# Moving small vector work of a two-layer network to POOL and ACT, and normalising attention for all heads at once

## The chip, the cores and the metric

The kernel runs on one core of a Trainium2 chip. Its engines work side by side, each through its own queue in a fixed order: TensorE (PE), VectorE (DVE), ScalarE (ACT), GpSimd (POOL) and SyncE (SP, which here issues most of the DMAs). They wait for each other through semaphores. The metric is the device time of one launch in microseconds. A time is a median of several runs; beside it stands one execution taken with the hardware profiler, from which all durations of single instructions come.

## The reference

Input x is 4 sequences of 512 tokens with 128 features, float32. Four blocks follow, each added to x after a layer norm:

```
x = x + L0_attn(layernorm(x))   # Mamba block, then causal attention (4 heads of 32, 2 KV heads), then gated FFN
x = x + L0_ffn(layernorm(x))    # 128 -> 512 with ternary weights, gelu, layer norm over 512, 512 -> 128
x = x + L1_attn(layernorm(x))   # a second Mamba block
x = x + L1_ffn(layernorm(x))    # router over 8 experts, top 1, gated FFN of width 512
```

A Mamba block projects to 2 x 256 channels, runs a convolution over 4 tokens, computes `delta = softplus(...)`, B and C, and then the selective scan over time for 16 states of each of 256 channels: `h = exp(delta * A) * h + delta * B * x`, `y = sum over states of h * C`. Then y is gated with `silu(z)` and projected back.

The norms: `layernorm(x) = (x - mean) / sqrt(var + 1e-5)`, `rmsnorm(x) = x / sqrt(mean(x^2) + 1e-6)`. Attention is `softmax(q k^T * scale, causal) v`.

## The kernel before

Four sequences (b = 0 to 3) are worked on as 4 tiles of 128 tokens each. The stages of a sequence are generators: `front0` (two norms, convolution, gate, B/C, softplus), `scan0` (16 jobs, each of two states of one half of the channels), `first` (back projection and attention), `dense` (gated FFN, then `bitffn` with ternary weights), `front1` and `scan1` for the second Mamba block, `second` (back projection and router), and then `sort` and `experts` for the sequences (0, 1), (2) and (3). `run` gives every stage a due time and `collect` draws steps from the generators in order of these.

Nothing is issued at once. Every call on an engine goes to `Plan.call`, which notes it with a cost from `Plan.cost` and its dependencies. `Plan.order` then lays out the queues of all engines: it takes, again and again, the instruction that can start first by its own model of time (within 0.1 us, the one that is due first), with room in the buffer rings taken into account and 1.35 us for a change of ACT's function table. `issue` emits the program in that order. So other operations or costs give another order in every queue. All planned instructions show as line 201 of the profile (the helper that emits them); the table loads are line 336, the scatters of rows line 1093.

A scan job (`scan_states`): PE spreads a row of B over all partitions into PSUM (`b_n<-parts,sel`), DVE multiplies it by `du` (`b_n<-b_n,du`), ACT makes the decay (`decay<-delta,nega`), DVE runs the scan (`hs<-decay,b_n`), POOL multiplies by C (`hs<-hs,rep`) and, in the first layer and for b below 2 in the second, adds the two states (`hs<-hs`); PE sums over states (`y<-hs,ident`). The decay has three buffers, `hs` four, the PSUM ring `mm` four.

The parts that the change touches:

- Norms: `moments` takes mean and variance on DVE, `rstd` raises `var + eps` to the power -1/2 on POOL, `shifted` makes the offset `-mean * r` on DVE (`nm_r<-mv,r`) and applies both on ACT. `two_norms` chains two of these, with three small DVE products (`ms`, `rr`) between.
- The end of `front`: B and C rows are split in bf16 parts (`parts`, `rest`), with a cast on DVE. Then softplus of v is computed as max(v, 0) plus log(1 + e) with e = exp(-|v|), where the logarithm is held within bounds that come from e. The tile `v` is `du` before `du` is made.
- `attention`: for the tile groups (0, 1), (2), (3) and each head, scores, row maximum, exponential, transposes to `tp`, copy to `pT`, product with v into `tp`, whose last column is the sum of the weights (`v` holds a column of ones); then, head by head, a reciprocal `rs` and a product into `o`.
- `bitffn`: gelu on ACT into `g`, its moments on DVE, and the norm over 512 features.

Of the kernel before, what the change touches and what calls it, by code (L numbers as in the profile page):

```python
# [14 lines left out]
AF = mybir.ActivationFunctionType  # L15
ALU = mybir.AluOpType
# [4 lines left out]
P = 128  # L21
B, T, D = 4, 512, 128
NT = T // P
# [3 lines left out]
HEADS, HD = 4, 32  # L27
FFN = 341
FCH = [(0, 128), (128, 128), (256, 85)]
HID, NHC = 512, 4  # L30
# [8 lines left out]
SCL, OFF, PROB, NUM = D, D + 1, D + 2, D + 3  # L39
# [311 lines left out]
class Net:  # L351
# [250 lines left out]
        self.nc.sync.dma_start(out=self.x[b], in_=self.a["x"][b].rearrange("(t p) d -> p t d", p=P))  # L602


    def rstd(self, name, var, eps, r=None):
        nc = self.nc
        r = self.sm("r", [P, NT], bufs=4) if r is None else r
        ve = self.sm("ve", [P, NT], bufs=4)
        nc.gpsimd.tensor_scalar(ve, var, eps, None, ALU.add)
        nc.gpsimd.tensor_tensor(r, ve, self.nhalf, ALU.pow)  # L610
        return r

    def moments(self, name, parts):

        nc = self.nc
        mv = self.sm("mv", [P, NT, 2], bufs=4)
        for t, part in enumerate(parts):
            st = self.sm("st", [P, 6], bufs=4)
            nc.vector.bn_stats(st, part)
            nc.vector.bn_aggr(mv[:, t, :], st)  # L620
        return mv

    def shifted(self, y, x, mean, r, off=None):

        nc = self.nc
        off = self.sm("nm_r", [P, NT], bufs=4) if off is None else off
        nc.vector.scalar_tensor_tensor(off, mean, -1.0, r, ALU.mult, ALU.mult)
        for t in range(NT):
            nc.scalar.activation(
                y[:, t, :], x[:, t, :], AF.Identity, bias=off[:, t:t + 1], scale=r[:, t:t + 1]  # L630
            )
        return y

    def layernorm(self, name, x):
        mv = self.moments(name, [x[:, t, :] for t in range(NT)])
        return self.shifted(self.t4("ln"), x, mv[:, :, 0], self.rstd(name, mv[:, :, 1], 1e-5))

    def two_norms(self, x):

        nc = self.nc  # L640
        mv = self.moments("in", [x[:, t, :] for t in range(NT)])
        r = self.rstd("in", mv[:, :, 1], 1e-5)
        ms = self.sm("ms", [P, NT])
        nc.vector.tensor_tensor(ms, r, r, ALU.mult)
        nc.vector.tensor_tensor(ms, ms, mv[:, :, 1], ALU.mult)
        rr = self.rstd("m", ms, 1e-6)
        nc.vector.tensor_tensor(rr, rr, r, ALU.mult)
        y = self.shifted(self.t4("ln"), x, mv[:, :, 0], rr)
        return self.shifted(self.t4("h", bufs=4), x, mv[:, :, 0], r), y

    def rmsnorm(self, name, x):
        nc = self.nc
        ss = self.sm("ss", [P, NT], bufs=4)
        y = self.t4("ln")
        for t in range(NT):
            nc.scalar.activation(y[:, t, :], x[:, t, :], AF.Square, scale=D ** -0.5, accum_out=ss[:, t:t + 1])
        r = self.rstd(name, ss, 1e-6)
        for t in range(NT):
            nc.scalar.activation(y[:, t, :], x[:, t, :], AF.Identity, scale=r[:, t:t + 1])
        return y  # L660
# [15 lines left out]
    def front(self, b, layer, x, scale=None):  # L676

        nc = self.nc
# [41 lines left out]
        rest = self.ft("rest", [P, T], tag="f", bufs=2)  # L720
        nc.scalar.copy(parts, ps)
        nc.vector.tensor_tensor(rest[64:, :], ps[64:, :], parts[64:, :], ALU.subtract)
        nc.vector.tensor_copy(parts[64:, :], rest[64:, :])
        nc.vector.tensor_tensor(parts[96:, :], rest[96:, :], parts[96:, :], ALU.subtract)

        yield
# [4 lines left out]
        for c in range(NB):  # L731
            ps = self.mm("dl_ps")
            for i in range(NB):
                nc.tensor.matmul(
                    ps, lhsT=step[:, i, c * P:(c + 1) * P], rhs=xs[:, i, :],
                    start=(i == 0), stop=(i == NB - 1),
                )
            nc.scalar.activation(v[:, c, :], ps, AF.Identity, bias=db[:, c:c + 1])
            nc.scalar.activation(e[:, c, :], ps, AF.Abs, bias=db[:, c:c + 1])
        yield  # L740
        nc.scalar.activation(e, e, AF.Exp, scale=-1.0)
        nc.scalar.activation(delta, e, AF.Ln, bias=1.0)
        nc.vector.scalar_tensor_tensor(v, v, 0.0, e, ALU.max, ALU.add)
        nc.gpsimd.tensor_tensor(delta, delta, e, ALU.subtract)
        nc.vector.scalar_tensor_tensor(e, e, -0.5, e, ALU.mult, ALU.mult)
        nc.vector.scalar_tensor_tensor(delta, delta, 0.0, e, ALU.min, ALU.max)
        nc.gpsimd.tensor_tensor(delta, v, delta, ALU.add)
        nc.gpsimd.tensor_tensor(du, delta, xs, ALU.mult)
        yield
        self.m[b] = xs, sz, delta, du, parts, cd  # L750
# [94 lines left out]
    def attention(self, b):  # L845
        nc = self.nc
        h = self.h[b]
        x = self.rmsnorm("a", h)
        xT = self.transposed(x, self.vec("norm_a"))
        qT = self.ft("qT", [P, T], bufs=1)  # L850
        ps = self.mm("q_ps")
# [14 lines left out]

        o = self.ft("o", [P, NT, D], bufs=1)
        turned = []
        for tiles in ((0, 1), (2,), (3,)):
            for hd in range(HEADS):  # L870

                hp, g = slice(hd * HD, (hd + 1) * HD), hd // 2
                at = [0, 1][:len(tiles)]
                ps = self.mm("s_ps")
                pr = self.ft("pr", [P, T], bufs=4)
                nm = self.sm("nm", [P, 2], bufs=4)
# [18 lines left out]
                turned.append(last)  # L895
                pT = self.ft("pT", [P, T], bufs=4)
                nc.scalar.copy(pT[:, :blocks * P], tp[:, :blocks * P])
                w = HD + 1
                for n, i in enumerate(tiles):
                    for j in range(i + 1):  # L900
                        nc.tensor.matmul(
                            tp[:, n * w:(n + 1) * w], lhsT=pT[:, (at[n] + j) * P:(at[n] + j + 1) * P],
                            rhs=v[:, j, g, :], start=(j == 0), stop=(j == i),
                        )
                m = len(tiles)
                po = tp[:, :m * w].rearrange("p (n w) -> p n w", w=w)
                rs = self.sm("rs", [P, 2, 1], bufs=4)
                nc.vector.reciprocal(rs[:, :m, :], po[:, :, HD:])
                nc.vector.tensor_tensor(
                    o[:, tiles[0]:tiles[0] + m, hp], po[:, :, :HD],  # L910
                    rs[:, :m, :].to_broadcast([P, m, HD]), ALU.mult,
                )
                yield
        oT = self.transposed(o)
        ps = self.mm4("oproj_ps")
        for t in range(NT):
# [5 lines left out]
    def ffn(self, b):  # L922
        nc = self.nc
        h = self.h[b]
        xT = self.transposed(self.rmsnorm("f", h), self.vec("norm_f"))
        hT = self.big("hT", [P, len(FCH), T])
        for i, (f0, fn) in enumerate(FCH):
            pg = self.mm("gate_ps")
            nc.tensor.matmul(pg[:fn, :], lhsT=self.wg[:, f0:f0 + fn], rhs=xT, start=True, stop=True)
            pu = self.mm("up_ps")  # L930
            nc.tensor.matmul(pu[:fn, :], lhsT=self.wu[:, f0:f0 + fn], rhs=xT, start=True, stop=True)
            sg = self.ft("sg", [P, T], bufs=1)
            nc.scalar.activation(sg[:fn, :], pg[:fn, :], AF.Silu)
            nc.vector.tensor_tensor(hT[:fn, i, :], sg[:fn, :], pu[:fn, :], ALU.mult)
        yield
        ps = self.mm4("down_ps")
        for t in range(NT):
            for i, (f0, fn) in enumerate(FCH):
                nc.tensor.matmul(
                    ps[:, t, :], lhsT=hT[:fn, i, t * P:(t + 1) * P], rhs=self.wd[:fn, i, :],  # L940
                    start=(i == 0), stop=(i == len(FCH) - 1),
                )
        nc.vector.tensor_tensor(h, h, ps, ALU.add)
        nc.gpsimd.tensor_tensor(self.x[b], self.x[b], h, ALU.add)
        yield

    def bitffn(self, b):
        nc = self.nc
        xT = self.transposed(self.layernorm("b", self.x[b]))
        g = self.big("gelu", [P, NT, HID])  # L950
        for t in range(NT):
            ps = self.mm("fc_ps")
            nc.tensor.matmul(ps, lhsT=xT[:, t * P:(t + 1) * P], rhs=self.wfc, start=True, stop=True)
            nc.scalar.activation(g[:, t, :], ps, AF.Gelu)
        yield
        mv = self.moments("h", [g[:, t, :] for t in range(NT)])
        r = self.rstd("h", mv[:, :, 1], 1e-5)
        self.shifted(g, g, mv[:, :, 0], r)
        gT = self.big("geluT", [P, NHC, T])
        lw, lb = self.vec("lnw"), self.vec("lnb")  # L960
        for c in range(NHC):
            tp = self.mm("tp")
# [14 lines left out]


    def front1(self, b):
        x = self.layernorm("s", self.x[b])  # L980
        yield
        yield from self.front(b, 1, x)

# [7 lines left out]
    def route(self, b):  # L991
# [8 lines left out]
            )  # L1000
        hot, hb = (t[:, ts] for t in self.choice)
        x, row = self.x[b], self.rows_x[b]
        mv = self.moments("e", [x[:, t, :] for t in range(NT)])
        r = self.rstd("e", mv[:, :, 1], 1e-5, row[:, :, SCL])
        ln = self.shifted(self.t4("ln"), x, mv[:, :, 0], r, row[:, :, OFF])
        xT = self.transposed(ln)
        ps = self.mm4("router_ps")
        for t in range(NT):
# [324 lines left out]
```

## Time and profile before

| | |
|---|---|
| median of 3 runs | 954.47 us (954.31 to 960.29) |
| the profiled execution | 953.64 us |
| its span, first to last instruction | 951.8 us |
| mean granted PE clock | 0.874 |
| PE busy | 768.1 us (81%), 3198 matmuls |
| DVE busy | 704.9 us (74%), 1149 instructions |
| POOL busy | 586.9 us (62%), 406 |
| ACT busy | 526.8 us (55%), 916, of them 57 table loads with 73.1 us |
| DMA | 108.70 MB, mean 114 GB/s |

Busy shares are means over stages with different limits; a matmul's end is modelled, so a busy PE is not PE at its peak. In a group's row stand the line, engine and operation, what is written and read, the shapes and the count, then busy time and the mean of one in ns, then the idle time of the engine just before these instructions and what ended it. A stretch row gives start and end, its length, and the busy time and number of instructions of each engine in it, then the granted PE clock and the DMA share. "Idle before" on an engine that is not the bottleneck costs nothing.

### The profile page before, as it was taken

The numbers are of one execution on the slowest core, as the hardware profiler recorded it, in microseconds if no ns is written. First come the engines' busy times: TensorE is split into PE (matmuls) and PEld (weight loads), VectorE is DVE, ScalarE is ACT, GpSimd is POOL, SyncE is SP. The second block draws the span as 40 slices with busy tenths as digits, with TensorE's granted clock in tenths as the row PEclk, the third lists the DMA queues.
The fourth block names the chain that finished last, engine by engine and source line by source line (L and its number), as shares of the span: only waits on it lengthen the run. The fifth ranks groups of instructions, "written<-read, shape, count | busy, mean of one in ns | idle before, by whom it ended". The sixth has DMA issues, their size and how long they took to land. (4 is left out here: it accounts for less than half of the span.)

```text
span 951.8 us, 10451 instructions
## 1 busy us (share of the span) xinstructions
PE 768.1 (81%) x3198; PEld 444.9 (47%) x3225; DVE 704.9 (74%) x1149; ACT 526.8 (55%) x916; POOL 586.9 (62%) x406
## 2 busy tenths in 40 slices
PE   4965669987999887889679998966798988889296
PEld 2411135444544644347225456433345666567185
DVE  5389996688778995787993857599978788787222
ACT  4572346545677565566546756683447556462142
POOL 4279987378666873747792535569758555563222
PEclk9965769978998999789969977978899999799689
DMA  5533343033221221412231204223425797575103
GB/s 164 156 108 110 116 128 111 2 104 109 75 89 46 89 95 38 133 45 67 90 134 43 67 23 155 90 85 129 141 74 188 242 322 244 176 243 183 41 23 93
DMA packets 52694, 108.70 MB, mean 114 GB/s; under 512 B 7700, under 2 KB 21748, under 8 KB 52639
## 3 DMA queue, kind: packets, MB, share of 16 engines
q1 hardware_dynamic: 50942, 105.90, 34.9%
q0 software_dynamic: 1696, 2.14, 0.7%
q8 instruction: 25, 0.41, 0.2%
q14 instruction: 31, 0.25, 0.1%
HBM read 103.12 MB, written 6.27 MB: 115 GB/s over the span
## 5 line engine op out<-in xcount | busy, mean ns | idle before, releaser
L201 POOL TENSOR_TENSOR hs<-hs,rep 128x1024 f32<-128x1024 f32 x126 | 299.4, 2377 | 148.1 <-issue 54.4
L201 DVE TENSOR_TENSOR_SCAN hs<-decay,b_n 128x512 f32<-128x512 f32 x256 | 311.7, 1218 | 18.2 <-ACT decay L201 1.7
L201 ACT ACTIVATE decay<-delta,nega 128x511 f32<-128x511 f32 x256 | 178.3, 718 | 155.7 <-DVE hs L201 146.5
L201 PE MATMUL y<-hs,ident 128*128 128x512 f32 x320 | 194.6, 711 | 20.4 <-POOL hs L201 19.6
L201 DVE TENSOR_TENSOR b_n<-b_n,du 128x512 f32<-128x512 f32 x256 | 173.9, 681 | 31.2 <-PE b_n L201 12.8
L201 PE MATMUL b_n<-parts,sel 128*128 128x512 bf16 x229 | 95.4, 446 | 89.2 <-DVE hs L201 83.2
L201 POOL TENSOR_TENSOR hs<-hs 128x512 f32<-128x512 f32 x96 | 123.3, 1285 | 7.1
L201 PEld LDWEIGHTS y<-hs,ident 128*128 128x128 f32 x320 | 63.0, 218 | 123.7 <-POOL hs L201 91.4
L1093 POOL DMA_INDIRECT out<-yj,xg x37 | 39.3, 1061 | 57.5 <-DVE yj L201 49.9
L336 ACT ACT_TABLE_LOAD x57 | 73.1, 1283 | 1.7 <-PEq L1322 0.8
L201 PEld LDWEIGHTS <-sel 128*128 128x128 bf16 x256 | 28.3, 111 | 84.0 <-issue 81.2
L201 PE MATMUL conv_ps<-xpad,taps 128*128 128x512 f32 x128 | 61.5, 622 | 0.7 <-ACT xpad L201 0.7
L201 DVE TENSOR_TENSOR sa<-sa,g_ps 128x512 f32<-128x512 f32 x37 | 25.1, 680 | 42.4 <-PE g_ps L201 39.6
L201 PEld LDWEIGHTS tp<-v,pT 128*128 128x128 f32 x320 | 44.2, 206 | 25.9 <-ACT pT L201 14.8
L201 PE MATMUL s_ps<-kT,qT 32*128 32x128 f32 (+3 forms) x128 | 54.5, 506 | 0.2 <-ACT kT L201 0.2
L201 DVE TENSOR_REDUCE nm<-s_ps 128x1 f32<-128x128 f32 (+2 forms) x64 | 30.3, 485 | 24.7 <-PE s_ps L201 24.4
L201 ACT COPY pT<-tp 128x384 f32<-128x384 f32 (+1 forms) x48 | 24.5, 515 | 43.2 <-PE tp L201 42.6
L201 PE MATMUL tp<-v,pT 128*128 128x33 f32 x320 | 44.7, 283 | 1.4 <-ACT pT L201 1.2
L201 PE MATMUL w_ps<-w_last,sa 128*128 128x128 f32 x296 | 41.5, 278 | 0.8 <-DVE sa L201 0.6
L201 ACT ACTIVATE pr<-s_ps,nm 128x128 f32<-128x128 f32 (+2 forms) x64 | 31.5, 525 | 15.9 <-DVE nm L201 15.7
L201 ACT ACTIVATE xn<-xg 128x128 f32<-128x128 f32 x37 | 18.2, 492 | 38.4 <-DMA xg<-sorted 35.8
L201 PEld LDWEIGHTS w_ps<-w_last,sa 128*128 128x128 f32 x296 | 37.4, 192 | 4.4 <-DVE sa L201 1.6
(197 smaller groups left out, 1233.4 us busy)
## 6 DMA issues: line engine op xcount, KB each, us to landing
rep<-cd SPq DMA_DIRECT2D x128, 512.0 KB
w_part<-in_w_rows SPq DMA_DIRECT2D x62, 256.0 KB
w_last<-in_w_rows SPq DMA_DIRECT2D x37, 256.0 KB
w_both<-in_w_rows SPq DMA_DIRECT2D x6, 512.0 KB
xg<-sorted SPq DMA_DIRECT2D x37, 66.0 KB
sorted<-zero SPq DMA_DIRECT2D x3, 726.0 KB
x<-in_x SPq DMA_DIRECT2D x4, 256.0 KB
raw_cw<-in_cw_rows SPq DMA_DIRECT2D x2, 512.0 KB
```

The source lines that it names most:

```text
L201: emit = lambda: getattr(getattr(self.nc, engine), what)(*[real(v) for v in args], **{n: real(v) for n, v in k.items()})
L336: self.nc.scalar.preload_act_table_set(self.SETS[table])
L1093: put = self.plan.nc.gpsimd.indirect_dma_start(out=real(to), out_offset=bass.IndirectOffsetOnAxis(ap=real(index).bitcast(U32), axis=0), in ...
```

## The change

Offsets of norms and the small products between two norms are made on POOL, from a negated mean that `less` makes there. In softplus `v + e` and the difference move so that POOL has four large instructions, the square goes to ACT, the maximum with zero is taken by ACT's Relu, and one DVE instruction is left; a cast of `parts` moves from DVE to ACT. The gelu statistics come from ACT: the sum as the gelu's accumulator, the sum of squared deviations from a Square pass into `gT` as scratch. In attention, the products with v of all four heads of a tile group are made after the last head's weights, side by side in the last `tp`, followed by one reciprocal and one product. The planner's costs stay as they are; calls lose an unused name.

```diff
-    def rstd(self, name, var, eps, r=None):
+    def rstd(self, var, eps, r=None, scale=1.0):
...
-        nc.gpsimd.tensor_scalar(ve, var, eps, None, ALU.add)
+        nc.gpsimd.tensor_scalar(ve, var, scale, eps, ALU.mult, ALU.add)
         nc.gpsimd.tensor_tensor(r, ve, self.nhalf, ALU.pow)
...
+    def less(self, mean, scale=-1.0):
+        nm = self.sm("nmean", [P, NT], bufs=4)
+        self.nc.gpsimd.tensor_scalar(nm, mean, scale, None, ALU.mult)
+        return nm
+
-    def shifted(self, y, x, mean, r, off=None):
+    def shifted(self, y, x, nmean, r, off=None):
...
-        nc.vector.scalar_tensor_tensor(off, mean, -1.0, r, ALU.mult, ALU.mult)
+        nc.gpsimd.tensor_tensor(off, nmean, r, ALU.mult)
...
     def two_norms(self, x):
...
-        nc.vector.tensor_tensor(ms, r, r, ALU.mult)
-        nc.vector.tensor_tensor(ms, ms, mv[:, :, 1], ALU.mult)
-        rr = self.rstd("m", ms, 1e-6)
-        nc.vector.tensor_tensor(rr, rr, r, ALU.mult)
-        y = self.shifted(self.t4("ln"), x, mv[:, :, 0], rr)
-        return self.shifted(self.t4("h", bufs=4), x, mv[:, :, 0], r), y
+        nc.gpsimd.tensor_tensor(ms, r, r, ALU.mult)
+        nc.gpsimd.tensor_tensor(ms, ms, mv[:, :, 1], ALU.mult)
+        rr = self.rstd(ms, 1e-6)
+        nc.gpsimd.tensor_tensor(rr, rr, r, ALU.mult)
+        y = self.shifted(self.t4("ln"), x, nm, rr)
+        return self.shifted(self.t4("h", bufs=4), x, nm, r), y
...
         nc.vector.tensor_tensor(rest[64:, :], ps[64:, :], parts[64:, :], ALU.subtract)
-        nc.vector.tensor_copy(parts[64:, :], rest[64:, :])
+        nc.scalar.copy(parts[64:, :], rest[64:, :])
         nc.vector.tensor_tensor(parts[96:, :], rest[96:, :], parts[96:, :], ALU.subtract)
...
-            nc.scalar.activation(v[:, c, :], ps, AF.Identity, bias=db[:, c:c + 1])
+            nc.scalar.activation(v[:, c, :], ps, AF.Relu, bias=db[:, c:c + 1])
...
         nc.scalar.activation(e, e, AF.Exp, scale=-1.0)
         nc.scalar.activation(delta, e, AF.Ln, bias=1.0)
-        nc.vector.scalar_tensor_tensor(v, v, 0.0, e, ALU.max, ALU.add)
-        nc.gpsimd.tensor_tensor(delta, delta, e, ALU.subtract)
-        nc.vector.scalar_tensor_tensor(e, e, -0.5, e, ALU.mult, ALU.mult)
-        nc.vector.scalar_tensor_tensor(delta, delta, 0.0, e, ALU.min, ALU.max)
-        nc.gpsimd.tensor_tensor(delta, v, delta, ALU.add)
+        nc.gpsimd.tensor_tensor(v, v, e, ALU.add)
+        nc.gpsimd.tensor_tensor(delta, e, delta, ALU.subtract)
+        nc.scalar.activation(e, e, AF.Square, scale=0.5 ** 0.5)
+        nc.vector.scalar_tensor_tensor(delta, delta, 0.0, e, ALU.max, ALU.min)
+        nc.gpsimd.tensor_tensor(delta, v, delta, ALU.subtract)
         nc.gpsimd.tensor_tensor(du, delta, xs, ALU.mult)
...
         for tiles in ((0, 1), (2,), (3,)):
+            at, m = [0, 1][:len(tiles)], len(tiles)
+            weights = []
             for hd in range(HEADS):
...
                 pT = self.ft("pT", [P, T], bufs=4)
                 nc.scalar.copy(pT[:, :blocks * P], tp[:, :blocks * P])
-                w = HD + 1
-                for n, i in enumerate(tiles):
+                weights.append(pT)
+                if hd < HEADS - 1:
+                    yield
+            for n, i in enumerate(tiles):
+                for hd in range(HEADS):
+                    k = n * HEADS + hd
                     for j in range(i + 1):
                         nc.tensor.matmul(
-                            tp[:, n * w:(n + 1) * w], lhsT=pT[:, (at[n] + j) * P:(at[n] + j + 1) * P],
-                            rhs=v[:, j, g, :], start=(j == 0), stop=(j == i),
+                            tp[:, k * w:(k + 1) * w], lhsT=weights[hd][:, (at[n] + j) * P:(at[n] + j + 1) * P],
+                            rhs=v[:, j, hd // 2, :], start=(j == 0), stop=(j == i),
                         )
-                m = len(tiles)
-                po = tp[:, :m * w].rearrange("p (n w) -> p n w", w=w)
-                rs = self.sm("rs", [P, 2, 1], bufs=4)
-                nc.vector.reciprocal(rs[:, :m, :], po[:, :, HD:])
-                nc.vector.tensor_tensor(
-                    o[:, tiles[0]:tiles[0] + m, hp], po[:, :, :HD],
-                    rs[:, :m, :].to_broadcast([P, m, HD]), ALU.mult,
-                )
-                yield
+            m *= HEADS
+            po = tp[:, :m * w].rearrange("p (n w) -> p n w", w=w)
+            rs = self.sm("rs", [P, 2 * HEADS, 1], bufs=4)[:, :m]
+            nc.vector.reciprocal(rs, po[:, :, HD:])
+            nc.vector.tensor_tensor(
+                o[:, tiles[0]:tiles[-1] + 1, :].rearrange("p t (h d) -> p (t h) d", d=HD), po[:, :, :HD],
+                rs.to_broadcast([P, m, HD]), ALU.mult,
+            )
+            yield
...
     def bitffn(self, b):
...
-            nc.scalar.activation(g[:, t, :], ps, AF.Gelu)
+            nc.scalar.activation(g[:, t, :], ps, AF.Gelu, accum_out=sums[:, t:t + 1])
         yield
-        mv = self.moments("h", [g[:, t, :] for t in range(NT)])
-        r = self.rstd("h", mv[:, :, 1], 1e-5)
-        self.shifted(g, g, mv[:, :, 0], r)
         gT = self.big("geluT", [P, NHC, T])
+        nm = self.less(sums, -1.0 / HID)
+        ss = self.sm("ss", [P, NT], bufs=4)
+        for t in range(NT):
+            nc.scalar.activation(gT[:, t, :], g[:, t, :], AF.Square, bias=nm[:, t:t + 1], accum_out=ss[:, t:t + 1])
+        self.shifted(g, g, nm, self.rstd(ss, 1e-5, scale=1.0 / HID))
```

`layernorm` and `route` call `less`, `rstd` and `shifted` in the same way as `two_norms`.

More of the change, by code (lines that the diff above doesn't have):

```diff
@@ L608, in rstd, with moments @@
         ve = self.sm("ve", [P, NT], bufs=4)
-        nc.gpsimd.tensor_scalar(ve, var, eps, None, ALU.add)
+        nc.gpsimd.tensor_scalar(ve, var, scale, eps, ALU.mult, ALU.add)
         nc.gpsimd.tensor_tensor(r, ve, self.nhalf, ALU.pow)
         return r
-    def moments(self, name, parts):
+    def moments(self, parts):
         nc = self.nc
@@ L632, in shifted, with layernorm, rmsnorm @@
         return y
-    def layernorm(self, name, x):
-        mv = self.moments(name, [x[:, t, :] for t in range(NT)])
-        return self.shifted(self.t4("ln"), x, mv[:, :, 0], self.rstd(name, mv[:, :, 1], 1e-5))
+    def layernorm(self, x):
+        mv = self.moments([x[:, t, :] for t in range(NT)])
+        nm = self.less(mv[:, :, 0])
+        return self.shifted(self.t4("ln"), x, nm, self.rstd(mv[:, :, 1], 1e-5))
     def two_norms(self, x):
         nc = self.nc
-        mv = self.moments("in", [x[:, t, :] for t in range(NT)])
-        r = self.rstd("in", mv[:, :, 1], 1e-5)
+        mv = self.moments([x[:, t, :] for t in range(NT)])
+        nm = self.less(mv[:, :, 0])
+        r = self.rstd(mv[:, :, 1], 1e-5)
         ms = self.sm("ms", [P, NT])
-        nc.vector.tensor_tensor(ms, r, r, ALU.mult)
-        nc.vector.tensor_tensor(ms, ms, mv[:, :, 1], ALU.mult)
-        rr = self.rstd("m", ms, 1e-6)
-        nc.vector.tensor_tensor(rr, rr, r, ALU.mult)
-        y = self.shifted(self.t4("ln"), x, mv[:, :, 0], rr)
-        return self.shifted(self.t4("h", bufs=4), x, mv[:, :, 0], r), y
-    def rmsnorm(self, name, x):
+        nc.gpsimd.tensor_tensor(ms, r, r, ALU.mult)
[4 more added lines that the diff above has]
+        return self.shifted(self.t4("h", bufs=4), x, nm, r), y
+    def rmsnorm(self, x):
         nc = self.nc
@@ L656, in rmsnorm @@
             nc.scalar.activation(y[:, t, :], x[:, t, :], AF.Square, scale=D ** -0.5, accum_out=ss[:, t:t + 1])
-        r = self.rstd(name, ss, 1e-6)
+        r = self.rstd(ss, 1e-6)
         for t in range(NT):
@@ L847, in attention @@
         h = self.h[b]
-        x = self.rmsnorm("a", h)
+        x = self.rmsnorm(h)
         xT = self.transposed(x, self.vec("norm_a"))
@@ L868, in attention @@
         turned = []
+        w = HD + 1
         for tiles in ((0, 1), (2,), (3,)):
+            at, m = [0, 1][:len(tiles)], len(tiles)
+            weights = []
             for hd in range(HEADS):
-                hp, g = slice(hd * HD, (hd + 1) * HD), hd // 2
-                at = [0, 1][:len(tiles)]
+                hp = slice(hd * HD, (hd + 1) * HD)
                 ps = self.mm("s_ps")
@@ L924, in ffn @@
         h = self.h[b]
-        xT = self.transposed(self.rmsnorm("f", h), self.vec("norm_f"))
+        xT = self.transposed(self.rmsnorm(h), self.vec("norm_f"))
         hT = self.big("hT", [P, len(FCH), T])
@@ L948, in bitffn @@
         nc = self.nc
-        xT = self.transposed(self.layernorm("b", self.x[b]))
+        xT = self.transposed(self.layernorm(self.x[b]))
         g = self.big("gelu", [P, NT, HID])
+        sums = self.sm("ss", [P, NT], bufs=4)
         for t in range(NT):
@@ L979, in front1 @@
     def front1(self, b):
-        x = self.layernorm("s", self.x[b])
+        x = self.layernorm(self.x[b])
         yield
@@ L1002, in route @@
         x, row = self.x[b], self.rows_x[b]
-        mv = self.moments("e", [x[:, t, :] for t in range(NT)])
-        r = self.rstd("e", mv[:, :, 1], 1e-5, row[:, :, SCL])
-        ln = self.shifted(self.t4("ln"), x, mv[:, :, 0], r, row[:, :, OFF])
+        mv = self.moments([x[:, t, :] for t in range(NT)])
+        nm = self.less(mv[:, :, 0])
+        r = self.rstd(mv[:, :, 1], 1e-5, row[:, :, SCL])
+        ln = self.shifted(self.t4("ln"), x, nm, r, row[:, :, OFF])
         xT = self.transposed(ln)
```

## The prediction

> **What bounds the kernel now.** I read the page's busy row first: VectorE 74%, PE 81%, GpSimd (POOL) 62%, ScalarE (ACT) 55% of 951.8 us. No engine is full, so the question is who paces which stretch. The stretch view cuts the span at places where the busy engine changes:
>
> ```profile
> core 0: us, PE busy (x) PEld busy (x) DVE busy (x) ACT busy (x) POOL busy (x), PEclk, DMA share, GB/s
> 48.00:144.00 96.00, 60.71 (x113) 21.38 (x112) 89.56 (x98) 43.98 (x71) 85.07 (x50) 0.65 0.35 113
> 144.00:192.00 48.00, 44.48 (x173) 23.18 (x174) 29.72 (x53) 28.69 (x53) 26.04 (x14) 0.96 0.17 56
> ...
> 408.00:504.00 96.00, 77.97 (x304) 40.38 (x304) 83.06 (x123) 56.35 (x104) 73.48 (x45) 0.84 0.26 88
> 504.00:624.00 120.00, 111.78 (x453) 65.56 (x455) 78.65 (x162) 78.67 (x135) 55.78 (x39) 0.90 0.23 76
> 624.00:696.00 72.00, 49.26 (x167) 25.91 (x167) 67.70 (x96) 35.90 (x55) 57.66 (x34) 0.79 0.37 120
> ```
>
> See two kinds of stretch in turn. In 48-144, 192-240, 288-360, 408-504 and 624-696 (384 us) the scans run and DVE is nearly full. In 144-192, 240-288, 360-408, 504-624 and 696-864 (432 us: attention, projections, experts) PE is busy 387.7 us, 90%, and DVE only 310.7. Start (48 us) and tail (88 us) are neither.
>
> Then the groups: who is full in a scan job?
>
> ```profile
> L201 POOL TENSOR_TENSOR hs<-hs,rep 128x1024 f32<-128x1024 f32 x126 | 299.4, 2377 | 148.1 <-issue 54.4
> L201 DVE TENSOR_TENSOR_SCAN hs<-decay,b_n 128x512 f32<-128x512 f32 x256 | 311.7, 1218 | 18.2 <-ACT decay L201 1.7
> L201 DVE TENSOR_TENSOR b_n<-b_n,du 128x512 f32<-128x512 f32 x256 | 173.9, 681 | 31.2 <-PE b_n L201 12.8
> L201 POOL TENSOR_TENSOR hs<-hs 128x512 f32<-128x512 f32 x96 | 123.3, 1285 | 7.1
> ```
>
> One job is two products and two scans on DVE, 2 x (0.681 + 1.218) = 3.80 us, and on POOL one product and, in 96 of 128 jobs, one sum: 2.377 + 1.285 = 3.66 us. POOL is almost as full as DVE. The timeline of POOL shows it without a gap:
>
> ```profile
> 477.44 2.35 POOL L201 TENSOR_TENSOR hs<-hs,rep 128x1024 f32<-128x1024 f32 x1
> 479.87 1.27 POOL L201 TENSOR_TENSOR hs<-hs 128x512 f32<-128x512 f32 x1
> 481.09 2.36 POOL L201 TENSOR_TENSOR hs<-hs,rep 128x1024 f32<-128x1024 f32 x1
> 483.53 1.27 POOL L201 TENSOR_TENSOR hs<-hs 128x512 f32<-128x512 f32 x1
> ```
>
> 481.09 - 477.44 = 3.65 us a job. The change takes work from DVE and gives some to POOL, so in scan stretches POOL is late next, in the others PE. That is why I credit only part of what leaves DVE.
>
> **The change part by part.** Rows of the groups by shape that carry the prices:
>
> ```profile
> L201 DVE SCALAR_TENSOR_TENSOR sp_e<-sp_e 128x1024 f32<-128x1024 f32 x8 | 12.8, 1603 | 2.8 <-POOL delta L201 2.8
> L201 DVE SCALAR_TENSOR_TENSOR du<-du,sp_e 128x1024 f32<-128x1024 f32 x8 | 11.4, 1428 | 4.7 <-ACT sp_e L201 4.7
> L201 DVE BATCH_NORM_STATS2 st<-gelu 128x6 f32<-128x512 f32 x16 | 10.6, 664 | 0.0
> L201 DVE SCALAR_TENSOR_TENSOR nm_r<-mv,r 128x4 f32<-128x4 f32 x20 | 8.8, 459 | 2.0 <-POOL r L201 1.7
> L201 DVE CAST parts<-rest 64x512 bf16<-64x512 f32 x8 | 6.8, 854 | 0.3
> L201 DVE RECIPROCAL rs<-tp 128x1 f32<-128x1 f32 x32 | 5.2, 163 | 13.2 <-PE tp L201 6.3 <-PE s_ps L201 3.8 <-ACT decay L201 2.8
> L201 DVE RECIPROCAL rs<-tp 128x2 f32<-128x2 f32 x16 | 2.6, 163 | 21.8 <-PE tp L201 16.9 <-ACT sz L201 4.9
> ```
>
> *Softplus, 8 times.* Two 128x1024 instructions leave DVE: 11.4 + 12.8 = 24.2 us. POOL gains v+e, priced by its row delta<-du,delta without blocking, 2.35 us: 8 x 2.35 = 18.8. ACT gains the square, by its exponential of the same shape 1.05: 8.4. Relu for Identity costs nothing more, both being one pass over 128x512 (0.687 us row). In the first batch, which nothing covers, the old chain after the exponential (end 40.0) was logarithm, POOL to 43.5, two DVE instructions to 46.1, POOL. The new one has POOL 40.0 to 44.7 (two instructions, the logarithm beside the first), ACT 1.05, DVE 1.22, POOL at 47.2: 1.1 us later. The new ACT wait has scan decays queued behind it; these are three buffers ahead and already wait 146.5 us for DVE, so it is covered; uncovered it would cost DVE some 1 us each, 8 in all.
>
> *Cast of parts, 8 times.* DVE loses 6.8 us, ACT gains 8 x 0.587 = 4.7. The next DVE subtraction now waits for ACT, with the scan's products behind it. The like wait, rest for ACT's parts, cost DVE 15.8 us over four occurrences; the price lies between 0 and 15.8, and I take 5, so this edit is about even.
>
> *Norms.* From DVE go 20 + 4 offsets, 12 small products: 8.8 + 0.6 + 1.3 + 1.8 = 12.6 us (459 ns is a mean; the tile view has median 161, maximum 2336). POOL gains 20 negated means at 0.23 (its 128x4 TENSOR_SCALAR row) and 36 products of 128x4, which the trace lacks. Bounds: 0.18, where a line through 128x512 (1.268) and 128x1024 (2.352) meets zero elements, and 1.04, the power of the same shape. A product is nearer the line: 0.2. Sum 4.6 + 7.2 = 11.8 us; at the upper bound 42.
>
> *Gelu statistics.* DVE loses 10.6 + 16 x 0.182 = 13.5 us. ACT gains 16 accumulator reads at 0.188 = 3.0, and 16 squares of 128x512 with bias and accumulator: between 0.602 + 0.188 (plain pass) and 0.804 + 0.188 (two column operands), I take 0.89: 14.2 us. POOL now waits twice on ACT per batch instead of once on DVE; behind it are scan products, then PE's y. The like wait, ve for mv, cost 36.0 us over 20 norms, 1.8 each; four more are 0 to 7 us, cover being POOL's slack of such stretches.
>
> *Attention.* 48 reciprocals and 48 products (7.8 + 9.7 = 17.5 us) become 12 and 12. The product rows 191 ns at 32 elements and 224 at 64 give 1.03 ns per element: 8 x 0.29 + 4 x 0.42 = 4.0, with 12 x 0.165 = 2.0. DVE saves 11.5 us. PE does the same matmuls later and in bursts; four pT buffers are all held until the fourth head is done, but the first three PSUM tiles come free after ACT's copy. The 35.0 us that DVE idled ahead of rs fall, but mostly turn into waits elsewhere, since PE was working then.
>
> No DMA is added or moved; what is pushed about on SP's queue is only order. The planner uses the costs to lay out every queue anew; table loads (57 x 1.283 = 73.1 us of ACT) may change by a few.
>
> **Sum.** DVE -68.6 us, POOL +30.6, ACT 8.4 + 4.7 + 17.2 = +30.3, PE 0. By stretch the tile views put 30.5 of DVE's saving in scan stretches, 33 in PE stretches, 5 in start and tail. For each scan stretch I take the fullest engine before and after:
> - 48-144: DVE 89.6 to 83.3, POOL 85.1 to 88.1: saves 1.5.
> - 192-240: DVE 40.7 to 39.6, POOL 38.7 to 38.9: 1.1.
> - 288-360: DVE 63.9 to 54.9, POOL 54.6 to 57.9, but PE 63.0: 0.9.
> - 408-504: DVE 83.1 to 73.5, POOL 73.5 to 77.1, PE 78.0: 5.1.
> - 624-696: DVE 67.7 to 63.2, POOL 57.7 to 60.9: 4.5.
>
> That is 13.1. In PE stretches only the 44.3 us in which PE was not busy can shrink; DVE loses 10.7% of its work there, so I take 4.7 (bounds 0 and 33). The start loses 1.1. Net 16.7: 953.6 - 16.7 = 936.9 for the profiled execution (span 951.8 plus 1.8 around it); the median of the runs is 0.8 higher, so **937**.
>
> **A rule against the change.** The Trainium skill, "GPSIMD Engine Reference", section Engine selection, says that two-input elementwise work belongs on VectorE, GpSimd being about twice as slow. The row agrees on price: 2.35 us against a DVE median of 1.24 (tile view), mean 1.43. By the rule alone the moved v+e costs 8 x (2.35 - 1.43) = 7.4 us more, and the forecast would be 944 plus whatever POOL delays. The trace decides by place: in 144-192 POOL sits 22 us of 48 idle, but in 48-144 only 11 of 96. I keep the rows' sum, and use the rule as the seed of the slower rival.
>
> **Rivals.**
> *POOL becomes the pace (slower), 972.* For it: 3.66 against 3.80 us a job, and 85.1 of 96. It decides once POOL's load in a scan stretch exceeds DVE's old one, or where its in-order waits hold scan products. Price: about 11 us added in scan stretches count in full, and four gelu waits 7: 954.5 + 18 = 972. Against it: DVE's saving in three of five such stretches exceeds POOL's gain. Chance 0.25.
> *PE hides it, 950.* Only 48-144, 192-240 and the little of 288-360 come: 954.5 - 3.5 - 1. For it: PE busy 90% in half the span. Against: 408-504 and 624-696 have PE under DVE. Chance 0.20.
> *DVE's queue was the pace everywhere, 906.* 70% of 68.6 comes through, as the shorter queue also removes the idle ahead of rs: 954.5 - 48. Against: POOL at 3.65 us without a gap. Chance 0.15.
> The forecast has 0.40.
>
> **Numbers.** About 1% is what a measurement here tells from no change. Faster by over 1%: 0.40 + 0.15 = 0.55; within: 0.20; slower: 0.25. The range 898 to 976 takes in the forecast and all rivals; with the small POOL product at half its upper bound (15 us more) the forecast would be 952, still inside.
>
> **What would show it.** Right: DVE near 636 us, POOL near 617, ACT near 557; rs 12 times with little idle; small POOL products near 0.2 us; POOL still at 3.65 us a job in scan stretches, those of 408-504 and 624-696 shorter. Wrong: POOL products of 128x4 near 1 us, or more idle before POOL's hs and PE's y; PE stretches that shrink by tens of us, which would make DVE the pace there; a table load count well off 57.

## The result, and the profile after

The changed kernel takes 964.69 us (median of 20 runs, 957.75 to 975.57), the kernel before 956.12 us in 20 runs beside it: a ratio of 1.0065, 95% interval 1.0039 to 1.0090. (A few disturbed runs count in the medians, but are left out of every ratio, of the comparison of orders and of the estimate for the clock below.) So it is slower by less than the 1% that I had called the least difference to be told apart; the interval excludes any gain. The forecast was 937.

First the busy row of the page after: engine, busy us, share of the span of 955.7 us, instructions.

```profile
PE 783.3 (82%) x3199; PEld 450.4 (47%) x3225; DVE 645.7 (68%) x985; ACT 545.8 (57%) x978; POOL 609.7 (64%) x470
```

DVE fell by 59.2 us (forecast 68.6), POOL rose by 22.8 (forecast 30.6), ACT by 19.0 (forecast 30.3). The work went where it was meant to go, and the span is 3.9 us longer. One term had no forecast at all: PE's busy time rose by 15.2 us, with the same instructions (3198 of them recorded before, 3199 after). The largest of its rows, before and after:

```profile
L201 PE MATMUL y<-hs,ident 128*128 128x512 f32 x320 | 194.6, 711 | 20.4 <-POOL hs L201 19.6
L201 PE MATMUL y<-hs,ident 128*128 128x512 f32 x320 | 202.8, 737 | 23.5 <-POOL hs L201 23.0
```

Median and maximum of this row did not move (592 and 1222 ns both times); more of its matmuls were long ones. The granted PE clock fell from 0.874 to 0.860. This comes back below.

The groups by shape show the new operations:

```profile
L201 POOL TENSOR_TENSOR du<-du,sp_e 128x1024 f32<-128x1024 f32 x8 | 18.8, 2354 | 12.4 <-ACT sp_e L201 12.4
L201 POOL TENSOR_TENSOR nm_r<-nmean,r 128x4 f32<-128x4 f32 x20 | 3.8, 201 | 1.3
L201 ACT ACTIVATE geluT<-gelu,nmean 128x512 f32<-128x512 f32 x16 | 11.4, 712 | 1.7 <-POOL nmean L201 1.7
L201 ACT ACTIVATION_READ_ACCUMULATOR geluT<-gelu,nmean 128x1 f32 x16 | 3.0, 189 | 0.0
L201 DVE RECIPROCAL rs<-tp 128x4 f32<-128x4 f32 x8 | 1.5, 182 | 16.4 <-PE tp L201 16.2
L201 DVE RECIPROCAL rs<-tp 128x8 f32<-128x8 f32 x4 | 0.8, 201 | 4.2 <-PE tp L201 2.8 <-PE s_ps L201 1.5
```

See the prices: v+e 2.354 us, the small POOL product 201 ns (taken at 0.2 between 0.18 and 1.04), the gelu square 0.712 + 0.189 (taken at 0.89). The idle ahead of `rs` fell from 35.0 to 20.6 us. But now the stretches, in the same columns as before:

```profile
48.00:144.00 96.00, 64.07 (x117) 22.42 (x116) 86.60 (x96) 46.90 (x77) 85.84 (x55) 0.62 0.41 126
144.00:192.00 48.00, 45.28 (x174) 23.35 (x176) 27.22 (x39) 31.92 (x58) 30.39 (x17) 0.98 0.20 67
...
408.00:504.00 96.00, 77.61 (x287) 43.26 (x288) 66.01 (x86) 51.16 (x97) 66.32 (x43) 0.79 0.26 88
504.00:624.00 120.00, 108.31 (x418) 63.20 (x421) 67.14 (x121) 76.62 (x139) 64.80 (x52) 0.84 0.25 80
624.00:696.00 72.00, 54.41 (x173) 25.94 (x174) 62.71 (x91) 43.22 (x74) 58.93 (x39) 0.81 0.33 117
```

The third number after the length is DVE. In 408-504 it fell from 83.1 to 66.0 us of 96, more than the 9.6 us forecast there; POOL also fell there, from 73.5 to 66.3. (The same 96 us need not hold the same work in both kernels: PE has 304 matmuls in them before, 287 after.) PE, with 77.6 us, is now the fullest engine of that stretch, no engine is near full, and yet the kernel is not shorter. DVE waits instead. Who it waits for (us, times, longest), the longest rows after:

```profile
DVE nm L201 <- PE s_ps L201: 68.6, 43, 6.3
DVE sa L201 <- PE g_ps L201: 38.4, 14, 13.8
DVE rs L201 <- PE tp L201: 19.0, 7, 7.5
DVE b_n L201 <- PE b_n L201: 18.9, 11, 5.1
```

The first of them before:

```profile
DVE nm L201 <- PE s_ps L201: 24.4, 29, 2.9
```

So 44 of the 59 us that left DVE stand here as idle time. Idle time is not yet lost time; what it costs is asked below.

### The profile page after: what moved, and what is told of

The parts are those of the page before. It is cut to its first block, busy times and chain, and to the rows that moved or that the text cites. A ratio compares the mean times of both kernels' runs of the same rounds, so it can differ in the third digit from the quotient of the medians.

```text
span 955.7 us, 10374 instructions
## 1 busy us (share of the span) xinstructions
PE 783.3 (82%) x3199; PEld 450.4 (47%) x3225; DVE 645.7 (68%) x985; ACT 545.8 (57%) x978; POOL 609.7 (64%) x470
## 5 line engine op out<-in xcount | busy, mean ns | idle before, releaser
L201 POOL TENSOR_TENSOR hs<-hs,rep 128x1024 f32<-128x1024 f32 x126 | 298.4, 2370 | 125.5 <-issue 40.1
L201 PE MATMUL y<-hs,ident 128*128 128x512 f32 x320 | 202.8, 737 | 23.5 <-POOL hs L201 23.0
L201 PE MATMUL b_n<-parts,sel 128*128 128x512 bf16 x230 | 97.7, 456 | 75.6 <-DVE hs L201 72.8
L201 DVE TENSOR_REDUCE nm<-s_ps 128x1 f32<-128x128 f32 (+2 forms) x64 | 30.6, 486 | 69.8 <-PE s_ps L201 68.6
L201 PE MATMUL s_ps<-kT,qT 32*128 32x128 f32 (+3 forms) x128 | 61.6, 564 | 0.0
L201 ACT COPY pT<-tp 128x384 f32<-128x384 f32 (+1 forms) x48 | 24.4, 516 | 47.4 <-PE tp L201 47.3
L201 PEld LDWEIGHTS w_ps<-w_last,sa 128*128 128x128 f32 x296 | 38.7, 196 | 8.0 <-issue 4.2
L201 ACT ACTIVATE xn<-xg 128x128 f32<-128x128 f32 x37 | 17.8, 490 | 35.8 <-DMA xg<-sorted 35.7
```

What stands on the lines that cost most here:

```text
L201: emit = lambda: getattr(getattr(self.nc, engine), what)(*[real(v) for v in args], **{n: real(v) for n, v in k.items()})
```

## The experiments

All times are medians; "before" stands for the kernel before, run beside each experiment, 954.7 to 956.2 us. Ratios are estimated from the runs, so a ratio can differ a little from that of two medians. My theories at the start were two of the rivals (PE hides the saving; POOL becomes the pace), and a third, "layout", which the planner suggests: it lays out all queues anew from the operations, so the change did not edit an order, it drew another one.

### One part of the change at a time

Each kernel has the operations of one part of the diff and nothing else of it.

**Attention alone** (`weights`, one `rs` and one product per tile group).

> Only the attention part of the change: one reciprocal and one product for all heads of a tile group; the rest as before. Theory PE (PE hides what leaves DVE in the attention stretches): 11.5 us leave DVE where PE is busy 90%, so 950 to 957. Theory attention (the batched heads are what costs: in the changed kernel DVE idles 68.6 us ahead of nm for s_ps instead of 24.4): 962 or more, with the idle ahead of nm over 50 us. Theory layout (any edit makes the planner lay out all queues anew, and two layouts differ by 1% whatever the edit is worth): anything from 945 to 970, unrelated to the 11.5 us.

Measured 1006.63 us, ratio 1.0557 [1.0527, 1.0587]. The idle ahead of `nm` is 53.4 us. This is what theory attention had expected.

**Softplus and cast alone.**

> Only the softplus part and the cast of parts on ACT. DVE loses 24.2 + 6.8 us, POOL gains 18.8, ACT 13.1. Theory PE: 948 to 955 (a few us in scan stretches). Theory POOL (POOL is the pace of scan stretches, so its added work counts): 960 to 966. Theory layout: 945 to 970, unrelated to these sums.

Measured 975.76 us, ratio 1.0182 [1.0120, 1.0244].

**Norms alone** (`less`, `shifted`, `two_norms` on POOL).

> Only the norms' small steps on POOL. DVE loses 12.6 us, POOL gains 12. Theory PE: 950 to 956. Theory POOL: 958 to 966. Theory layout: 945 to 970, unrelated to these sums.

Measured 978.09 us, ratio 1.0241 [1.0221, 1.0262].

**Gelu statistics alone.**

> Only the gelu statistics on ACT. DVE loses 13.5 us in stretches where PE is busy, ACT gains 17. Theory PE: 952 to 957. Theory POOL (waits of POOL for ACT hold the scan products): 958 to 964 with idle ahead of nmean and ve above 30 us. Theory layout: 945 to 970, unrelated to these sums.

Measured 978.47 us, ratio 1.0238 [1.0197, 1.0279]. Idle of POOL ahead of `nmean` and `ve` sums to 40.8 us here (11.3 + 9.6 + 9.5 + 7.8 + 2.6). That is above the 30 us of theory POOL, but so was the 41.2 ahead of `ve` before (36.0 + 2.7 + 2.5): theory POOL has no new wait to point to in these rows.

Four parts, 1.8 to 5.6% slower each, and together 0.65% slower. The last three lie above every range that I had given, that of theory layout too. No fixed price per part adds up to this: the norms' 12.6 us of small DVE steps can't cost 23 us alone and nothing beside the other parts. It points to the layout, which is another one in each kernel, but does not show it.

### The same operations in other orders

The edit is one constant of the planner; the instructions stay the same, the queues do not.

```diff
-    SWITCH = 1.35
+    SWITCH = 1.30
```

Kernel before with 1.30, 1.40, 1.25 and 1.45:

> Nothing of the change: the kernel before, with the planner's constant for a change of ACT's table 1.30 instead of 1.35. The same instructions, other queue orders. Theory layout (the order of before is a fortunate one, picked with its constants, and any other order costs 1 to 3%): 965 to 985. Theory parts (each of the four parts was slower alone for its own operations): 950 to 959, as nothing is moved.

> The kernel before with the same constant at 1.40. Theory layout: 965 to 985. Theory parts: 950 to 959.

> The kernel before with the planner's table constant at 1.25. Theory layout (before is an outlier): 970 to 995. If 1.30 and 1.40 were unlucky instead: 950 to 965.

> The kernel before with the planner's table constant at 1.45. Theory layout: 970 to 995. If 1.30 and 1.40 were unlucky: 950 to 965.

Measured 992.51, 984.73, 978.64 and 969.13 us: ratios 1.0379 [1.0337, 1.0421], 1.0321 [1.0272, 1.0370], 1.0235 [1.0202, 1.0268] and 1.0131 [1.0094, 1.0168]. Not one comes within 13 us of the 955.7 of the kernel before. Busy row of the slowest, 1.30:

```profile
PE 804.3 (81%) x3225; PEld 462.6 (47%) x3225; DVE 709.0 (72%) x1149; ACT 528.8 (53%) x916; POOL 590.1 (60%) x406
```

DVE, ACT and POOL have the same counts as before and within some 4 us the same work, over a span of 990.6 instead of 951.8 us. PE shows 36 us more; some 12 of these are only 27 matmuls that the trace of before lacks (it has 229 of 256 `b_n<-parts,sel`, 446 ns each), the other 24 are the same matmuls taking longer. Changes of ACT's table do not explain it: 57, as many as before; the 984.73 has 53. The rival ranges, from 950 to 959 or 965, are missed by 4 to 34 us; theory layout, which expected 965 to 985 twice and 970 to 995 twice, has two of the four inside, one 7.5 us above and one 1 us below.

Changed kernel with 1.25, 1.30 and 1.45:

> The changed kernel with the same constant at 1.25. Theory layout: the changed operations are worth some 15 us beside a like layout of the old ones, so 945 to 970 here where the perturbed kernel before gives 965 to 985. Theory parts: 958 to 972, as nothing else is moved.

> The changed kernel with the same constant at 1.30. Theory layout: 945 to 970. Theory parts: 958 to 972.

> The changed kernel with the same constant at 1.45. Theory layout with operations worth some 25 us: 940 to 970. If the operations are worth nothing beside layouts of before: 970 to 995.

Measured 941.36, 960.43 and 960.03 us: ratios 0.9840 [0.9808, 0.9871], 1.0009 [0.9979, 1.0039] and 1.0031 [0.9998, 1.0063]. With 1.25 the changed kernel beats both kernels of this case, though it has the most table loads of all (63 x 1.283 = 80.8 us of ACT). Its busy row, beside the changed kernel's own above:

```profile
PE 772.9 (82%) x3225; PEld 451.6 (48%) x3225; DVE 645.7 (69%) x985; ACT 556.8 (59%) x986; POOL 609.3 (65%) x470
```

DVE and POOL are equal to 0.4 us, ACT is even busier by 11, and it is 23 us faster. The instructions are the same, so this comes from the order, with all that the order brings. PE's matmuls are among that: its busy time is 10 us less, and 22 us less once the 26 matmuls that the trace with 1.35 lacks are added (12 us). The 960.43 lies where both theories had it and decides nothing; the 941.36 is below both; the 960.03 lies where theory layout had it.

Taken together, old operations with a constant not their own: 969.1, 978.6, 984.7, 992.5, mean 981.2, standard deviation 9.9. Changed operations in all four orders, counted as said at the start: 941.4, 955.2, 959.4, 962.6, mean 954.6, standard deviation 9.4. The difference is 26.6 us; with four of each, and if the constants count as random draws, its 95% interval is about 17 us either side (2.45 x root of (9.9 squared + 9.4 squared) / 4). So beside orders of their kind the changed operations save some 10 to 43 us, and the 16.7 of the forecast lies inside. The kernel before, though, stands 25.5 us below the other orders of its operations. It is left out of their mean as the one order that was in use, and whether it had been picked for its time no run tells; counted in, the difference is 21.5 us with 19 either side. The changed kernel's own order lies 8.0 us above the mean of its kind. By these means 955.7 + 25.5 - 26.6 + 8.0 = 962.6 is where the changed kernel stands; that is bookkeeping, for every term comes from the same medians, and no check of them.

**The clock of PE** moves with the orders, and no run holds it fixed. The mean granted clock is 0.871 in the runs of the kernel before and 0.866, 0.854, 0.863, 0.844 in its other orders (1.45, 1.25, 1.40, 1.30); it is 0.861 in the changed kernel and 0.877, 0.867, 0.862 with 1.25, 1.30, 1.45. Slower orders tend to have the lower clock. How much of the time is that? Two estimates. Over 83 runs of the kernel before, which all have one order and clocks between 0.866 and 0.881, 0.01 less clock goes with 1.7 us more, and loosely so: the 0.010 between the two kernels would be some 2 us, the 0.027 of the slowest order some 5 of its 37 us. Or by PE's busy time, at the 0.36 us per us that is measured further below: 15.2 us more would be 5 us, and the 24 us of the slowest order 9. So the clock is a part of what an order is worth, and by both estimates not the whole. The stretch rows suggest that the order acts on the clock: in 48-144 of the kernel before PE is busy 61 of 96 us at a granted clock of 0.65, in 144-192 it is busy 44 of 48 at 0.96. Which of the two leads was not tried.

### Is attention's 1007 its order or itself?

> Only the attention part, constant at 1.30. If 1007 was its layout: 970 to 995. If the batched heads themselves cost: 1000 or more.

> Only the attention part, constant at 1.45. If 1007 was its layout: 970 to 995. If the batched heads themselves cost: 1000 or more.

Measured 991.55 and 1003.17 us, ratios 1.0343 [1.0276, 1.0409] and 1.0514 [1.0478, 1.0550]. One falls into each of the two ranges. With 1006.6 the mean of three is 1000.5, 19 us above the mean of old operations in other orders; the fastest of the three lies just below the slowest of the four, so the gap is likely, not certain. The wait table has a second mark, the idle of DVE ahead of `nm` (us, times, longest). Attention alone with 1.45:

```profile
DVE nm L201 <- PE s_ps L201: 58.8, 41, 6.9
```

Old operations with 1.25:

```profile
DVE nm L201 <- PE s_ps L201: 24.5, 28, 3.5
```

The same row in the other kernels: attention alone 53.4 us with 1.35 and 42.4 with 1.30 (longest 6.9 in both); old operations 24.4 with 1.35, 31.9 with 1.30, 22.2 with 1.40, 21.0 with 1.45 (longest 2.8 to 3.3); the whole change 68.6, 43.0, 57.8 and 53.5 with 1.35, 1.25, 1.30 and 1.45 (longest 6.3, 4.3, 6.4, 6.3). Heads one by one with another part changed lie between: softplus alone 44.6, norms alone 41.0, gelu alone 32.7 (longest 4.1, 3.6, 3.4). Two of these profiled executions took longer than the medians: 974.5 us for the whole change with 1.30, 981.6 for softplus alone. So the sums overlap a little, and they are no measure of the time: the fastest kernel of all, with 1.25, has 43.0 us of it. The longest single wait is 6.3 to 6.9 us in six of the seven kernels with batched heads, and 4.3 in the seventh; it is at most 4.1 in the eight with heads one by one. How one looks: the timeline after, PE and DVE around the longest.

```profile
151.29 1.21 DVE L201 TENSOR_TENSOR_SCAN hs<-decay,b_n 128x512 f32<-128x512 f32 x1
152.27 2.74 PE L201 MATMUL conv_ps<-xpad,taps 128*128 128x512 f32 x6
...
155.10 0.42 DVE L201 TENSOR_REDUCE nm<-s_ps 128x1 f32<-128x256 f32 x1 [2.60 <-PE s_ps L201]
...
157.00 1.88 PE L201 MATMUL conv_ps<-xpad,taps 128*128 128x512 f32 x4
...
158.72 1.88 PE L201 MATMUL y<-hs,ident 128*128 128x512 f32 x4
...
161.11 0.69 PE L201 MATMUL s_ps<-kT,qT 32*128 32x256 f32 x2
...
161.84 0.29 DVE L201 TENSOR_REDUCE nm<-s_ps 128x1 f32<-128x128 f32 x1 [6.31 <-PE s_ps L201]
```

From 152.5 to 161.84 DVE does one row maximum. The next one stands at the head of its queue, the scores that it needs stand on PE behind convolution and `y`, and no scan is ahead of it. Why batched heads make the planner put `nm` so early was not tried. Nor was the whole change without its attention part, so what batched heads cost inside the whole change is open: the parts do not add up. Beside the 981.2 attention alone stands at +19 us (mean of three orders), the other parts at -5, -3 and -3 (one order each), and the whole at -27 (mean of four).

### The order of before, kept to the instruction

Here the plan is made with the old operations and costs; only at emission something else is issued at the same place, for instance:

```diff
-        nc.vector.scalar_tensor_tensor(v, v, 0.0, e, ALU.max, ALU.add)
+        nc.vector.scalar_tensor_tensor(v, v, 0.0, e, ALU.max, ALU.add, swap=(
+            "gpsimd", lambda q: q.tensor_tensor(real(v), real(v), real(e), ALU.add)))
```

**Softplus and cast moved, at their old places.**

> The softplus part and the cast as in the change, but issued at the very places which these instructions have in the order of the kernel before: PE's and SP's queues are the same as before to the last instruction, DVE, ACT and POOL differ only by the 24 instructions that move. Theory layout: near the kernel before, 948 to 960, though the same edit with queues laid out anew gave 976. Theory parts (the operations themselves cost): 970 to 982 again.

Measured 975.55 us, ratio 1.0201 [1.0145, 1.0257]. This is the range of theory parts: my theory in its plain form ("the operations cost nothing, only a new order does") fell here. The groups of this kernel name the wait, busy and mean ns, then idle before:

```profile
L202 DVE SCALAR_TENSOR_TENSOR delta<-delta,sp_e 128x1024 f32<-128x1024 f32 x8 | 15.1, 1884 | 21.5 <-ACT sp_e L762 21.5
L762 ACT ACTIVATE sp_e<-sp_e 128x1024 f32<-128x1024 f32 x8 | 8.4, 1056 | 6.9 <-POOL delta L202 6.9
```

The place of the remaining DVE instruction was laid out for a chain with one POOL product before it. Now there are two, and DVE stands 21.5 us, 2.7 each of the 8 times, with products and scans behind it; before, its idle in that place was 0.3. The cast has a wait of its own, 6.8 us ahead of the subtraction into `parts`, 0.9 each time; before it was 0.3 in all.

**Only the square moved, at its old place**; the bound that it gives has the other sign in this kernel.

> The order of the kernel before, unchanged; of softplus only the square moves from DVE to ACT, at its place. The chain does not get longer (1.05 us on ACT for 1.22 on DVE), DVE loses 12.8 us. If the 976 of the whole softplus part at unchanged places came from its longer chain (one more POOL product of 2.35 us ahead of DVE's wait, 8 times): 950 to 957. If any moved instruction costs by its queue: 962 or more.

Measured 952.09 us, ratio 0.9969 [0.9954, 0.9983]: faster by 3 us. Its wait is shorter, and DVE has one 1.22 us instruction less ahead of it:

```profile
DVE delta L202 <- ACT sp_e L760: 11.9, 8, 3.4
```

So moving this instruction to another queue cost nothing; v+e on POOL, which makes the chain longer, or the cast makes the 976. The two were not separated by a run; the waits, 21.5 against 6.8 us, point to the first.

**DVE, PE and POOL lighter, nothing added** (in the first, Relu stands for Identity as well, one pass either way).

> The order of the kernel before, unchanged; two softplus instructions, the cast of parts and the statistics of gelu are computed on a small part of their columns only, so some 35 us leave DVE and nothing is added anywhere. If DVE is the pace: 920 to 930. Theory PE (PE hides most of it, as the forecast had it): 938 to 948. If DVE does not matter in this order: 950 to 956.

> The order of the kernel before, unchanged; the second to fourth taps of the convolution are multiplied for 128 of 512 columns only, so some 30 us leave PE. Theory PE: 925 to 938. If PE only looks busy: 946 to 956.

> The order of the kernel before, unchanged; the sum of two states is made for 320 of 512 columns only, so some 38 us leave POOL. If POOL is the pace of the scan stretches: 925 to 940. Otherwise 948 to 956.

Measured 949.64, 946.55 and 951.14 us, ratios 0.9934 [0.9897, 0.9972], 0.9885 [0.9834, 0.9937] and 0.9950 [0.9924, 0.9977]. Their busy rows:

```profile
PE 772.4 (82%) x3225; PEld 444.0 (47%) x3225; DVE 675.9 (71%) x1149; ACT 526.4 (56%) x916; POOL 581.5 (61%) x406
```

```profile
PE 752.1 (80%) x3225; PEld 445.0 (47%) x3225; DVE 705.4 (75%) x1149; ACT 525.5 (56%) x916; POOL 586.9 (62%) x406
```

```profile
PE 771.5 (82%) x3225; PEld 448.1 (47%) x3225; DVE 698.9 (74%) x1149; ACT 525.8 (56%) x916; POOL 548.2 (58%) x406
```

By the ratios, DVE lost 29.0 us for 6.3 us of time: 0.22 per us (0.09 to 0.34 by the interval). POOL lost 38.7 for 4.8: 0.12 (0.06 to 0.19). PE lost 96 x (0.592 - 0.275) = 30.4 us in its convolution rows (tile view, medians; the engine's busy sum fell by 16.0, or by 28 once the 27 matmuls that the trace of before lacks are added to it) for 11.0: 0.36 per us of those rows (0.20 to 0.52). For PE and POOL the time fell where I had it if the engine is not the pace, for DVE between two of the ranges. None of the three is the pace of this order; PE may be the nearest to it, but the intervals of PE and DVE overlap.

## Why the prediction was wrong, point by point

- **What bounds the kernel.** 16.7 of 68.6 us credited is 0.24 per us, and the order of before gives 0.22. The size agrees, but by luck, for the way to it was another: 13.1 of the 16.7 came from taking the fullest engine of each scan stretch as its pace, and the lighter kernels show none that is. 38.7 us less on POOL gave 4.8, and 30.4 less on PE gave 11.0. The gapless POOL timeline showed an engine that keeps up with its feeder, not one that sets the pace.
- **The prices** were right within 12 us per engine, but for PE. The gelu waits of POOL that I feared (36.0 us before ahead of `ve` for `mv`) came out as 9.1 us for `nmean` on `mv`, 8.8 on gelu and 16.2 for `ve` on ACT. "PE 0" held for the instructions and not for their time, which rose by 15.2 us.
- **Sums and readings.** 936.9 + 0.8 is 937.7, so the forecast's own sum is 938. By its list of stretches DVE's saving exceeds POOL's gain in all five, not in three. A small POOL product at half its upper bound (0.52 us) would add 36 x 0.32 = 11.5 us, not 15. None of this bears on the miss.
- **The step that failed** is the sentence "The planner uses the costs to lay out every queue anew; table loads may change by a few", priced at nothing. Table loads went from 57 to 55, as said. The new layout, though, is a term of its own: for unchanged operations it is worth +13 to +37 us, as the order of before lies 25.5 us under the mean of its kind. The changed kernel's order did not have that luck; it lies 8.0 above the mean of its kind. Put in afterwards, these two terms make the forecast's 937.7 into 971 with my 16.7 us for the operations; the rest of the way to the measured time is inside the 17 us by which the worth of the operations is uncertain.
- **The queue that waits longer** was the second thing missing: I priced the softplus chain as late only in the first batch, 1.1 us. At unchanged places DVE waits 2.7 us for it each of 8 times, in a kernel that is 19 us slower. When the planner may re-place it, that wait shrinks to 6.2 us in all, so in the changed kernel itself it is small.
- **Attention.** The 35.0 us ahead of `rs` "mostly turn into waits elsewhere": so they did, and more. Ahead of `rs` 14 us went, ahead of `nm` 44 came. I had counted 11.5 us of saving and no price. Alone, the part is likely to have one (+19 us beside the 981.2); in the whole change it is not shown.
- **The rivals.** "POOL becomes the pace" has little in the rows after: PE's `y` waits 23.0 us for POOL's `hs` instead of 19.6, while POOL's own idle ahead of `hs` fell from 148.1 to 125.5. "PE hides it", 950, is the nearest in kind, but it too took the new order for free, and PE is no full cover: 30.4 us less on it gave 11.0. The time fell into "within 1%", to which I had given 0.20, and not for the reason of that rival.

## What to carry to other kernels

Where a program derives the order of all queues from its costs, every edit is two edits: the operations, and a new draw of the order. Before an edit is judged, draw several orders of both versions by a constant that changes no instruction, and compare the groups; one order of each says little when orders of one kind spread by 21 to 23 us and the one in use may be a fortunate one. And an edit that wins by its operations can be taken further by searching its own orders: the best of four here gave 941.4 us, 1.6% under the kernel before.

## What the runs showed that I had not expected

At a fixed order 29 us taken from the fullest-looking engine of the scan stretches were worth 6 us, and 39 us from the second 5. A likely reading is that with four in-order queues that wait for each other time is lost at many small handovers; no run shows that by itself. The changed kernel's 20 runs spread over 17.8 us, those of before over 10.0; no run tells why, and it stays open.
